# More combined images, some direct images normalised by VectorE, and weight steps in even portions, in a grouped convolution after a group norm

## The chip, the cores and the metric

The kernel runs on one core of a Trainium2 chip. A core has TensorE (matmuls into PSUM; PE in the profile, with PEld for its weight loads), VectorE (DVE), ScalarE (ACT), GpSimd (POOL) and SyncE (SP), which here issues most DMA transfers. Each engine works through its own queue in order; semaphores tie the queues together. The metric is the device time of one execution in microseconds (us). Durations of single instructions come from one profiled execution.

## What is computed

```python
# x: (160, 128, 32, 32) f32;  U: (5, 128*128*9) f32
s1 = (U.max() - U.min()) / 3;  v1 = s1 * floor(U / s1)
s2 = s1 / 5;                   v2 = s2 * floor((U - v1) / s2)
w  = (v1 + v2).reshape(128 * 5, 128, 3, 3)

def gn(v):                     # 32 groups of 4 channels over an image
    g = v.reshape(B, 32, 4, H, W)
    return (g - mean(g)) / sqrt(var(g) + 1e-5)

xb  = gn(x).reshape(32, 5 * 128, 32, 32)
act = conv(xb, w, 3x3, stride 1, padding 1, groups=5)
out = x + act.reshape(160, 128, 32, 32)
```

So there are five weight sets; each is applied to 32 of the 160 images. Every image is normalised, convolved 3x3 over 128 channels, and added to itself.

## The kernel before, in words

The 128 channels lie on the partitions. The kernel takes the images set by set (`place`), two images to a chunk of `xpool`. Matmuls are in f16, with the f32 data split into a high and a low part so that precision is kept. Per image there are these stages:

- **Load and statistics.** SyncE loads a chunk `LOAD_LEAD` = 20 images ahead. ScalarE measures an image 14 ahead with two passes (`image_sum`, L192; `image_square`, L199); eight early images are measured by VectorE (`BY_VECTOR`). GpSimd and two tiny matmuls turn eight images' sums into `rstd` and `shift`.
- **Direct images** (even ones from image 8 on). ScalarE writes z = x·rstd + shift (L510), then the f16 high part hi (L518). VectorE writes the low part lo = z - hi (L573) and combines its rows: differences two rows apart, sums and differences of row pairs (`combinations`, L587, L589, L590). TensorE convolves hi with the nine taps (L613, 18 matmuls over 512 columns, about) and the combined rows of lo with four combined weights per column of taps (L651, 6 of 512 and 12 of 256).
- **Combined images** (odd ones from `STEADY` = 7 on). The row combinations are formed on the raw x in f32: the outer rows on GpSimd (`outer_rows`, L538, L539), the rest on VectorE (`combine`, L549, L552, L555), 2048 values per partition in v. ScalarE scales v into vh (L560), VectorE into vl = v·rstd - vh (L566). TensorE needs no direct taps: 12 matmuls of 512 columns and 24 of 256 (L651).
- **The pair sums m.** For either kind `sums_of_pairs` lets TensorE first write the products of row sums and row differences to m, two PSUM banks. ScalarE copies the second bank to SBUF (`leave`, L709). VectorE writes their sum and difference into the rows of the output accumulator eo (`pairs`, L719, L721), and TensorE adds the remaining products on top (`rest_of_column`). `ps_m` has one buffer, `ps_eo` two.
- **Output.** ScalarE halves eo into `sum` (L735); GpSimd issues a DMA that adds it to the image in SBUF (L748); SyncE stores the chunk (L753).

The weights of the next set are quantised by VectorE meanwhile: `make_column` is a generator whose 14 steps for each of the three columns are taken one by one (`take(later, 1)`), 42 in all, from the third image of a set to its 29th (for the first set, from the fifth).

The order of every queue is written out by hand in `run`. In iteration i of the main loop the queues get:

- TensorE: m of i+1, then the rest of image i;
- ScalarE: the first pass over a new image, the output sum of i-1, the copy of m(i+1), z and hi or vh of i+3, the second pass;
- VectorE: the low part of i+2, L719 and L721 for i+1 (with a step or the last of three row combinations between them), the combine of i+4, and a step of the weights;
- GpSimd: the DMA issue for i-1, the outer rows of i+4, pieces of the statistics and weights;
- SyncE: the store of the chunk that ends in i-2, and loads.

Of the kernel before, what the change touches and what calls it, by code (L numbers as in the profile page):

```python
# [8 lines left out]
F32 = mybir.dt.float32  # L9
I32 = mybir.dt.int32  # L10
MM = mybir.dt.float16
ALU = mybir.AluOpType
# [297 lines left out]
class Main:  # L310
# [22 lines left out]


    STAT_LEAD = 14
    LOAD_LEAD = 20
    STEADY = 7
    BY_VECTOR = (8, 10, 11, 14, 19, 24, 29, 34)
    EARLY = 8
    FIRST = 3  # L340

# [4 lines left out]
    def __init__(self, tc, ctx, keep, x, u, out):  # L346
        nc = self.nc = tc.nc
        self.imgs, C, self.H, self.W = x.shape
        P = self.P = nc.NUM_PARTITIONS
        assert C == P and self.H * self.W == 1024  # L350
        self.per_set = self.imgs // N_SETS
        self.xv = x.rearrange("(b n) c h w -> n c b (h w)", n=N_SETS)
        self.ov = out.rearrange("(b n) c h w -> n c b (h w)", n=N_SETS)
        self.uv = u.rearrange("n (o i k) -> n o i k", o=C, k=TAPS)

        def pool(name, bufs, **kw):
            return ctx.enter_context(tc.tile_pool(name=name, bufs=bufs, **kw))

        self.const = pool("const", 1)
        self.qpool = pool("quant", 1)  # L360
        self.wpool = pool("weights", 2)
        self.upool = pool("u", 1)
        self.xpool = pool("x", 12)
        self.zpool = pool("z", 3)
        self.parts = pool("parts", 5)
        self.rows = pool("rows", 4)
        self.wide = pool("wide", 1)
        self.wide_parts = pool("wide_parts", 2)
        self.evac = pool("evac", 2)
        self.sums = pool("sums", 4)  # L370
        self.unread = pool("unread", 1)
        self.small = pool("small", 3)
        self.ps_eo = pool("ps_eo", 2, space=PSUM)
        self.ps_m = pool("ps_m", 1, space=PSUM)
        self.ps_stat = pool("ps_stat", 1, space=PSUM)
        self.ps_tr = pool("ps_tr", 1, space=PSUM)
        self.steps = Steps(nc, keep)
        self.chunks, self.z, self.hi, self.v, self.eo, self.m = {}, {}, {}, {}, {}, {}
        self.sum = {}
        self.wts = {}  # L380
        self.columns = []

        cuts = [0, 2, 4, 8, 12, 16, 20, *range(24, self.imgs + 1, 8)]
        self.groups = [range(a, b) for a, b in zip(cuts, cuts[1:])]
        self.group_of = {i: k for k, g in enumerate(self.groups) for i in g}
        self.stats = {}
# [118 lines left out]
    def normalise(self, i):  # L505
# [7 lines left out]
        )  # L513
        self.z[i] = z

    def high_part(self, i):
        hi = self.parts.tile([self.P, self.H, self.W], MM, tag="hi", name=f"hi{i}")
        self.nc.scalar.copy(hi.rearrange("p h w -> p (h w)"), self.z[i])  # L518
        self.hi[i] = hi

    def combined(self, i):

        return self.STEADY <= i < self.imgs and i % 2 == 1

    def column_of(self, i):

# [230 lines left out]
    def run(self):  # L757
# [39 lines left out]
        def take(steps, count):  # L797
            for _ in range(count):
                next(steps, None)

        def measure(stage, *images):
            for i in images:
                self.measure(i, (stage,))
# [68 lines left out]
        later, turned = iter(()), []  # L872
        for i in range(self.imgs):
            n, b = self.place(i)


            def on_the_way(col):
                if col == self.COLS[1]:
                    for st in ready:
                        st.means()  # L880
                    for *column, parts in self.columns:
                        turned.append((column, self.turn_column(*column, parts)))
                    self.columns.clear()
                if col == self.COLS[2]:
                    for st in middle:
                        st.variances()

            if i < self.FIRST:
                if i == self.FIRST - 1:
                    self.sums_of_pairs(self.FIRST)  # L890

                j = (i - 1) % self.FIRST
                self.direct_hi(j, self.COLS[2])
                self.direct_lo(j, self.COLS[2])
                if i == 0:
                    self.stats[2].variances()
                    self.stats[2].deviation()
                    self.stats[2].scales()
                for col in self.COLS:
                    on_the_way(col)  # L900
            else:
                j = i - 1
                self.conv(i, on_the_way)
            ahead = i + min(10 + i // 4, self.STAT_LEAD + 1)
            to_measure = range(measured, min(self.imgs, ahead))
            measured += len(to_measure)
            if n + 1 < N_SETS:
                if b == (2 if n == 0 else 0):
                    self.load_set(n + 1)
                if b == (4 if n == 0 else 2):  # L910
                    later = (s for col in self.COLS for s in self.make_column(n + 1, col))
            by_scalar = [k for k in to_measure if not self.by_vector(k)]
            by_vector = [k for k in to_measure if self.by_vector(k)]

            if i < self.FIRST:

                if i == 0:
                    measure(0, 8, 9, 10)
                    self.normalise(4)
                    self.high_part(4)  # L920
                if i == 2:
                    self.leave(3)
                    self.normalise(5)
                    measure(1, 9)
                    self.high_part(5)
                    self.pairs(3)
                    self.low_part(4)
                    run(self.combinations(4))
                self.residual(j)
                if i == 1:  # L930
                    measure(0, 11)
            else:

                rows = iter(())
                if self.combined(i + 2):
                    self.low_combined(i + 2)
                elif i + 2 < self.imgs:
                    self.low_part(i + 2)
                    take(later, 1)
                    rows = self.combinations(i + 2)  # L940
                    take(rows, 2)
                if i > self.FIRST and self.by_hand(j):
                    self.residual(j)
                for k in by_scalar:
                    self.measure(k, (0,))
                if i > self.FIRST and not self.by_hand(j):
                    self.residual(j)
                    self.accumulate(j)
                if self.combined(i + 4):
                    self.outer_rows(i + 4)  # L950


                part = i + 3 < self.imgs and not self.combined(i + 3)
                if i + 1 < self.imgs:
                    self.leave(i + 1)
                if part:
                    self.normalise(i + 3)
                    self.high_part(i + 3)
                if self.combined(i + 3):
                    self.high_combined(i + 3)  # L960
                for k in by_scalar:
                    self.measure(k, (1,))
            for st in middle:
                st.deviation()
                st.scales()
            for st in ready:
                st.deviations()
            for column, pt in turned:
                self.keep_column(*column, pt)
            turned = []  # L970

            if i >= self.FIRST:

                if i + 1 < self.imgs:
                    self.pairs(i + 1, lambda: take(rows if i % 2 == 0 else later, 1))
                run(rows)
                if self.combined(i + 4):
                    self.combine(i + 4)
                else:
                    take(later, 1)  # L980
                if b == self.per_set - 4:
                    run(later)

            middle, ready = ready, []
            if i >= self.FIRST:
                measure(0, *by_vector)
            for k in to_measure:
                group = self.group_of[k]
                if k + 1 == self.groups[group].stop:
                    ready.append(self.stats[group])  # L990
            self.store(i - 2)
            while loaded * NB < min(self.imgs, i + self.LOAD_LEAD):
                self.load(loaded)
                loaded += 1
# [49 lines left out]
```

## Time and profile before

| | |
|---|---|
| time, median of 3 runs | 1002.48 us (1001.89 to 1003.06) |
| span of the profiled execution | 1000.1 us, TensorE clock at 0.999 of full speed |
| images combined / not combined | 77 / 83 |
| DMA traffic | 254.42 MB, mean 254 GB/s |
| load of a chunk, issue to landing | median 9.0 us |
| added output, issue to landing | median 6.9 us, longest 11.8 |

The main loop runs from about 60 us to 990 us of the span: 157 images, 5.92 us each. Busy time of an engine is the union of its instructions; instructions of one engine overlap by some tens of ns, so that starts, not durations, are to be added up. In the slices of the page a digit is a tenth of a slice of 25 us. A wait is shown as "waiting instruction <- what ended the wait: total, times, longest". In a timeline the number in brackets is the idle time of that engine just ahead of the instruction.

### The profile page before, as it was taken

What the parts mean: (1) busy time and instruction counts of PE and PEld (TensorE: products, weight loads), DVE (VectorE), ACT (ScalarE), POOL (GpSimd) and SP (SyncE); (2) the same over time, 40 slices, a digit from 0 to 9 for tenths busy, and PEclk for the clock granted to TensorE, in tenths of its full rate; (3) what the DMA queues carried; (4) which work ended last, traced back from release to release, by engine and by line L of the source; (5) the groups of instructions that cost most, each with busy time, mean ns of one, the idle gap of its engine ahead of it and who ended that gap; (6) DMA issues with size and microseconds to landing.
All of it is one profiled execution on the core that took longest, in us unless ns stands there. A gap on an engine that the chain in (4) does not pass through costs nothing.

```text
span 1000.1 us, 15977 instructions
## 1 busy us (share of the span) xinstructions
PE 962.5 (96%) x5935; PEld 575.1 (58%) x5935; DVE 895.6 (90%) x1237; ACT 913.2 (91%) x1243; POOL 405.3 (41%) x575
## 2 busy tenths in 40 slices
PE   1999999999999999999999999999999999999997
PEld 0445555565655565666655566666565666666554
DVE  7999999998999999989999998999999988888884
ACT  4879999999999999999999999999999999998560
POOL 3435473553425262524364443426353523233310
PEclk9999999999999999999999999999999999999999
DMA  9628989999999999999989999999999999988773
GB/s 357 247 89 229 257 221 279 269 268 267 272 273 269 266 258 273 288 274 269 264 243 288 270 265 278 277 273 249 266 272 270 279 262 275 274 230 219 177 179 141
DMA packets 67287, 254.42 MB, mean 254 GB/s; under 512 B 5248, under 2 KB 5248, under 8 KB 67200
## 3 DMA queue, kind: packets, MB, share of 16 engines
q1 hardware_dynamic: 45168, 173.09, 50.2%
q0 software_dynamic: 22032, 80.23, 41.4%
q8 instruction: 48, 0.79, 0.3%
q14 instruction: 39, 0.32, 0.1%
HBM read 89.19 MB, written 83.89 MB: 173 GB/s over the span
## 4 chain that ended last, share of the span: by engine, by line
PE 73%; DVE 10%; ACT 10%; issue 3%; POOL 3%; DMA 1%; SPq 0%; DVEq 0%; POOLq 0%
PE eo L613 25%; PE m L651 25%; PE eo L651 22%; ACT junk L199 2%; ACT vh L560 2%; ACT sum L735 1%; ACT m L709 1%; DVE eo L719 1%; DVE eo L721 1%; ACT z L510 1%; ACT junk L192 1%; DVE lo L573 1%; DVE vl L566 1%; DMA range<-in_L_conv_U_dram 1%; DVE ext L421 1%
## 5 line engine op out<-in xcount | busy, mean ns | idle before, releaser
L651 PEld LDWEIGHTS <-wt 128*128 128x128 f16 x4212 | 409.0, 98 | 241.3 <-DVE eo L721 12.9
L613 PE MATMUL eo<-hi,wt 128*128 128x496 f16 (+1 forms) x1476 | 352.5, 375 | 1.1 <-ACT wt L475 0.6
L748 POOL DMA_DIRECT2D xt<-sum x153 | 136.5, 895 | 419.4 <-ACT sum L735 403.5
L613 PEld LDWEIGHTS <-wt 128*128 128x128 f16 x1548 | 151.3, 99 | 147.4 <-ACT wt L475 1.8
L566 DVE SCALAR_TENSOR_TENSOR vl<-v,rstd,vh 128x2048 f16<-128x2048 f32 x77 | 180.8, 2348 | 4.2 <-ACT vh L560 4.2
L651 PE MATMUL m<-vh,wt 128*128 128x496 f16 (+1 forms) x462 | 175.7, 380 | 5.2 <-DVE eo L721 4.6
L719 DVE TENSOR_TENSOR eo<-m,m 128x512 f32<-128x512 f32 x157 | 109.0, 695 | 77.8 <-ACT m L709 77.8
L651 PE MATMUL eo<-vl,wt 128*128 128x256 f16 (+1 forms) x924 | 177.1, 273 | 0.0
L651 PE MATMUL eo<-vh,wt 128*128 128x256 f16 (+1 forms) x924 | 177.1, 273 | 0.0
L651 PE MATMUL m<-vl,wt 128*128 128x496 f16 (+1 forms) x462 | 175.4, 380 | 0.0
L199 ACT ACTIVATE junk<-xt,mv 128x1024 f16<-128x1024 f32 x152 | 174.0, 1145 | 0.2
L192 ACT ACTIVATE junk<-xt 128x1024 f16<-128x1024 f32 x152 | 160.6, 1057 | 14.7 <-DMA xt<-in_x_dram 11.6
L735 ACT ACTIVATE sum<-eo 128x1024 f32<-128x1024 f32 x153 | 154.1, 1007 | 13.7 <-PE eo L651 13.7
L560 ACT ACTIVATE vh<-v,rstd 128x2048 f16<-128x2048 f32 x77 | 155.0, 2013 | 1.8 <-POOL v L539 1.8
L651 PE MATMUL eo<-rows,wt 128*128 128x248 f16 (+1 forms) x960 | 144.3, 273 | 0.0
L651 PE MATMUL m<-rows,wt 128*128 128x496 f16 (+1 forms) x480 | 116.9, 380 | 0.5 <-DVE eo L721 0.5
L709 ACT COPY m<-m 128x512 f32<-128x512 f32 x157 | 91.3, 582 | 27.4 <-PE m L651 23.9
L721 DVE TENSOR_TENSOR eo<-m,m 128x512 f32<-128x512 f32 x157 | 108.4, 691 | 1.0
L510 ACT ACTIVATE z<-xt,shift,rstd 128x1024 f32<-128x1024 f32 x83 | 103.2, 1243 | 3.5 <-POOL shift L242 3.5
L573 DVE TENSOR_TENSOR lo<-z,hi 128x1024 f16<-128x1024 f32 x83 | 101.5, 1223 | 0.0
L518 ACT CAST hi<-z 128x1024 f16<-128x1024 f32 x83 | 86.8, 1046 | 2.6
L549 DVE TENSOR_TENSOR v<-xt 128x960 f32<-128x960 f32 x77 | 88.4, 1149 | 0.0
(111 smaller groups left out, 863.3 us busy)
## 6 DMA issues: line engine op xcount, KB each, us to landing
xt<-in_x_dram SPq DMA_DIRECT2D x78, 1024.0 KB, 9.0
out_dram<-xt SPq DMA_DIRECT2D x78, 1024.0 KB, 5.2
xt<-sum POOLq DMA_DIRECT2D x153, 512.0 KB, 6.9
range<-in_L_conv_U_dram SPq DMA_DIRECT2D x4, 576.0 KB, 7.9
u<-in_L_conv_U_dram SPq DMA_DIRECT2D x4, 576.0 KB, 11.8
xt<-in_x_dram SPq DMA_DIRECT2D x4, 512.0 KB, 10.6
out_dram<-xt SPq DMA_DIRECT2D x3, 512.0 KB, 2.7
u<-in_L_conv_U_dram SPq DMA_DIRECT2D x2, 288.0 KB, 3.0
```

Of the source, the lines that this page charges most:

```text
L192: self.nc.scalar.activation(junk, image, ACTF.Copy, scale=-1.0 / image.shape[1], accum_out=self.mv[:, j, 0:1],)
L199: self.nc.scalar.activation(junk, image, ACTF.Square, bias=self.mv[:, j, 0:1], accum_out=self.mv[:, j, 1:2],)
L510: nc.scalar.activation(z, self.image(i), ACTF.Identity, bias=st.shift[:, j : j + 1], scale=st.rstd[:, j : j + 1],)
L560: self.nc.scalar.mul(vh, self.v[i], st.rstd[:, j])
L566: self.nc.vector.scalar_tensor_tensor(vl, self.v[i], st.rstd[:, j], self.hi[i], ALU.mult, ALU.subtract)
L573: self.nc.vector.tensor_sub(lo[:, 1 : self.H + 1, :].rearrange("p h w -> p (h w)"), self.z.pop(i), self.hi[i].rearrange("p h w -> p (h w)"),)
L613: nc.tensor.matmul(target[:, h, r0 - h0 : r1 - h0, c0:c1], self.wts[n, col][:, k, :], tile[:, s0 : s0 + r1 - r0, c0 + dw : c1 + dw], start ...
L651: self.nc.tensor.matmul(target[:, :, c0:c1], self.wts[n, col][:, kind, :], source[:, :, c0 + dw : c1 + dw], start=start, stop=stop, skip_g ...
L719: nc.vector.tensor_add(rows[:, :, 0], m[:, 0], m2)
L721: nc.vector.tensor_sub(rows[:, :, 1], m[:, 0], m2)
L735: nc.scalar.mul(self.sum[i], eo, 0.5)
L748: self.nc.gpsimd.dma_start(self.image(i), self.sum.pop(i), accum_op=ALU.add)
```

## The change

More of the images take the combined form: instead of every second one, four of each seven up to image 125 (positions 0, 2, 4, 6 of the seven, so that two follow each other where sevens meet), and two of each three from image 126 on. That is for TensorE, which has fewer columns to stream in a combined image. Of the direct images that are left, one in seven up to image 125 and all from 126 on have z written by VectorE instead of ScalarE (27 in all), for ScalarE's sake. Weight steps are taken in even portions: beside those at fixed places, a count due at the end of each iteration is made up. Two combined images in a row need two `wide` buffers and three `wide_parts`; to make room the x pool goes from 12 chunks to 11 with a lead of 18, and `sums` from 4 to 3.

```diff
-    LOAD_LEAD = 20
+    LOAD_LEAD = 18
+    THIRDS = 126
...
-        self.xpool = pool("x", 12)
+        self.xpool = pool("x", 11)
...
-        self.wide = pool("wide", 1)
-        self.wide_parts = pool("wide_parts", 2)
+        self.wide = pool("wide", 2)
+        self.wide_parts = pool("wide_parts", 3)
...
-        self.sums = pool("sums", 4)
+        self.sums = pool("sums", 3)
...
+    def normalise_by_vector(self, i):
+        st, j = self.column_of(i)
+        z = self.z[i] = self.zpool.tile([self.P, 1024], F32, tag="z", name=f"z{i}")
+        self.nc.vector.tensor_scalar(
+            z, self.image(i), st.rstd[:, j], st.shift[:, j], ALU.mult, ALU.add
+        )
+
+    def by_vector_too(self, i):
+        if i < self.STEADY + 4 or i >= self.imgs or self.combined(i):
+            return False
+        return i >= self.THIRDS or (i - self.STEADY) % 7 == 3
...
     def combined(self, i):
-        return self.STEADY <= i < self.imgs and i % 2 == 1
+        if i < self.STEADY or i >= self.imgs:
+            return False
+        return (i - self.STEADY) % 7 % 2 == 0 if i < self.THIRDS else i % 3 != 1
...
+        def steps_due(b, first):
+            last = self.per_set - 5
+            return 0 if b < first else 42 * (b - first + 1) // (last - first + 1)
...
                 if part:
-                    self.normalise(i + 3)
+                    if not self.by_vector_too(i + 3):
+                        self.normalise(i + 3)
                     self.high_part(i + 3)
...
-                    self.pairs(i + 1, lambda: take(rows if i % 2 == 0 else later, 1))
+                    self.pairs(i + 1, lambda: take(later if self.combined(i + 2) else rows, 1))
                 run(rows)
                 if self.combined(i + 4):
                     self.combine(i + 4)
-                else:
-                    take(later, 1)
+                elif self.by_vector_too(i + 4):
+                    self.normalise_by_vector(i + 4)
+
+                take(later, steps_due(b, 4 if n == 0 else 2) - self.step)
```

More of the change, by code (lines that the diff above doesn't have):

```diff
@@ L380, in __init__ @@
         self.wts = {}
+        self.step = 0
         self.columns = []
@@ L799, in take, with counted @@
                 next(steps, None)
+        def counted(steps):
+            self.step = 0
+            for step in steps:
+                self.step += 1
+                yield step
+        def steps_due(b, first):
+            last = self.per_set - 5
+            return 0 if b < first else 42 * (b - first + 1) // (last - first + 1)
         def measure(stage, *images):
@@ L910, in run @@
                 if b == (4 if n == 0 else 2):
-                    later = (s for col in self.COLS for s in self.make_column(n + 1, col))
+                    later = counted(
+                        s for col in self.COLS for s in self.make_column(n + 1, col)
+                    )
             by_scalar = [k for k in to_measure if not self.by_vector(k)]
```

## The prediction

> **What bounds the kernel now.** First the busy table and the slices of the page, for the balance of the engines:
>
> ```profile
> PE 962.5 (96%) x5935; PEld 575.1 (58%) x5935; DVE 895.6 (90%) x1237; ACT 913.2 (91%) x1243; POOL 405.3 (41%) x575
> ...
> PE   1999999999999999999999999999999999999997
> ...
> DVE  7999999998999999989999998999999988888884
> ACT  4879999999999999999999999999999999998560
> ```
>
> TensorE, VectorE and ScalarE are all nearly full; VectorE has room only in the last slices, where no weights are made. Then the waits, to see who is late:
>
> ```profile
> DVE eo L719 <- ACT m L709: 77.8, 77, 2.0
> ...
> PEld L651 <- DVE eo L721: 12.9, 31, 1.5
> PE m L651 <- DVE eo L721: 5.0, 10, 1.2
> ```
>
> They form a ring. TensorE writes m(i+1); ScalarE copies half of it (L709); VectorE adds and subtracts (L719, L721); only then may TensorE write m(i+2), because `ps_m` has one buffer. So what counts is the rhythm from image to image. The timeline of one pair of images shows it (start, duration, engine, line, idle before):
>
> ```profile
> 511.06 0.39 PE L651 MATMUL m<-vh,wt 128*128 128x512 f16 x1 [0.17 <-DVE eo L721]
> ...
> 514.50 0.58 ACT L709 COPY m<-m 128x512 f32<-128x512 f32 x1
> ...
> 516.74 0.68 DVE L721 TENSOR_TENSOR eo<-m,m 128x512 f32<-128x512 f32 x1
> ...
> 518.79 1.46 PE L651 MATMUL m<-rows,wt 128*128 128x512 f16 x6
> ...
> 520.29 0.59 ACT L709 COPY m<-m 128x512 f32<-128x512 f32 x1
> ...
> 520.91 0.70 DVE L719 TENSOR_TENSOR eo<-m,m 128x512 f32<-128x512 f32 x1 [0.97 <-ACT m L709]
> ...
> 522.18 0.69 DVE L721 TENSOR_TENSOR eo<-m,m 128x512 f32<-128x512 f32 x1
> ```
>
> The next m starts at 522.92, 0.05 after VectorE's end: the pair takes 11.86 us, of which TensorE was held 0.17. Near 890 us, where no weights are made, a pair takes 11.64 (m starts at 889.15 and 900.79) with no stall.
>
> [...] 12 matmuls of m take 2.61 (511.06 to 513.67), 0.217 each, and L721 has a mean of 691. [...]
>
> **The change, part by part.** C is a combined image, D a direct one.
>
> TensorE. C needs 12 matmuls for m and 24 half-size ones: 2.60 + 2.66 = 5.26. D takes 1.30 for m and 5.12 for the rest (513.67 to 518.79): 6.42. There were 77 C, now 68 + 23 = 91: 14 x 1.16 = **16.2 us less TensorE work**.
>
> VectorE, start to start in the trace: combine (L549, L552, L555) 2.34; vl 2.28; lo and its three rows 1.13+0.60+0.33+0.33 = 2.39; the two ops on m 1.21; a weights' step 0.48 on average (14 rows of 0.34 to 0.75, less overlap). C costs 2.34+2.28-2.39 = 2.23 more than D: 14 x 2.23 = **31 us more**. The new z is an fp32 `tensor_scalar` from SBUF, 1024 wide, 27 times; no row shows it. [...] I take 0.65: 18 us more.
>
> ScalarE: 27 z at 1.24 go, 34 us; C costs 1.9 against 2.23 for z and hi. From one copy of m to the next it needs, start to start, copy 0.47, vh 1.90 (or z 1.28 + hi 0.95), square 1.27, sum 1.06, output sum (L735) 0.93: **5.68 for C, 6.0 for D**, 4.73 for D with z on VectorE.
>
> So per seven images: TensorE 4 x 5.26 + 3 x 6.42 = 40.3, VectorE 4 x 4.62 + 3 x 2.39 + 7 x 1.21 + 0.65 = 34.8, with 11 steps x 0.48 = 40.1, ScalarE 39.5. No total exceeds TensorE's, but VectorE has nothing left for waiting, and the order inside the seven matters.
>
> The ring, image by image. M = start of m(i+1) on TensorE, A = end of its copy, D = end of L721:
> - next M = later of M + P and D + 0.05. P is what TensorE has in iteration i, m(i+1) and then the rest of image i: 1.30 + 2.66 = 3.96 for C before D, 2.60 + 5.12 = 7.72 for D before C, 2.60 + 2.66 = 5.26 for C before C.
> - A = later of previous A + V (ScalarE's work between two copies, set by the kind of image i+2) and M + 2.1 where image i+1 is D (518.79 to 520.88), M + 3.4 where it is C (1.3 more matmuls).
> - D = later of previous D + W (VectorE's queue) and A + 1.33 + what stands between L719 and L721: a step 0.48 or rows 0.33.
>
> W holds, in the queue's order, combine(i+3) or z(i+3), the low part of i+2 (vl or lo with rows), the two ops on m, and 0.78 of steps (42 over 26 images, at 0.48). So combine+lo+ops is 5.94, vl+ops 3.49, combine+vl+ops 5.83, each plus 0.78. The sequence is C D C D C D C and again C, r = (i-7) mod 7. I start from M = 0 with the last A at -1.80 and the last D at -0.05, about where the table ends:
>
> | r | P | V | W | M | A | D |
> |---|---|---|---|---|---|---|
> | 0 | 3.96 | 5.68 | z+vl 4.92 | 0 | 3.88 | 5.69 |
> | 1 | 7.72 | 4.73 | 6.72 | 5.74 | 9.14 | 12.41 |
> | 2 | 3.96 | 5.68 | 4.27 | 13.46 | 15.55 | 17.36 |
> | 3 | 7.72 | 6.00 | 6.72 | 17.42 | 21.55 | 24.08 |
> | 4 | 3.96 | 5.68 | combine+vl 6.61 | 25.14 | 27.23 | 30.69 |
> | 5 | 7.72 | 5.68 | 4.27 | 30.74 | 34.14 | 35.95 |
> | 6 | 5.26 | 6.00 | 6.72 | 38.46 | 41.86 | 43.52 |
>
> The next M is 43.72. TensorE is held 1.78 after r0, since two copies after adjacent C come 3.96 apart and ScalarE needs 5.68, and 1.64 after r4, since VectorE has combine and vl in one short image. Before, 3.5 pairs took 41.5: **+2.2 per seven**. The same rules give 11.7 for the old pair (measured 11.86), so they do not exaggerate. Without steps they give 41.6 against 3.5 x 11.64 = 40.7: +0.9. With two of three combined the crossing comes every three images, with W = 2.34+2.28+1.21 = 5.83 where TensorE has 3.96: in the C before C iteration D is M + 3.4 + 1.33 + 0.33 = M + 5.06; the next D is 5.83 later, so the M after that cannot come before M + 10.94, where TensorE alone needs 5.26 + 3.96 = 9.22. The three take 16.94 + 1.72 = 18.66 against 1.5 x 11.64 = 17.46: **+1.2**.
>
> Sum: steps run during 99 of images 7 to 125, 14.1 sevens x 2.2 = +31; the other 20, 2.9 x 0.9 = +2.6; the end, some 10 threes x 1.2 = +12. Together +46: **1048**. The z estimate hardly enters[...].
>
> Costs put at nothing: the second `wide` and third `wide_parts` buffer serve adjacent C. `sums` 4 to 3: reuse comes three images later, 17 us; the transfer lands in 6.9 us, at most 11.8. `xpool` 11 and lead 18: issue to first use falls from five images to three, about 18 less 5 us of SP's lateness = 13; loads between 300 and 800 us land in 7.2 to 11.8. Hidden, narrowly. Even portions replace a burst of few steps: already in W.
>
> **The rivals.**
> 1. *TensorE stays the bound.* For it: the totals fit, and ScalarE is relieved. Then 16.2 go, and with them some 3 of the 17.9 us of waits shown above: 983. Against it: one m buffer cannot carry slack from long images into short ones. 12%.
> 2. *Half of the stalls.* If VectorE's steps happen to fall into the long images, the hold after r4 goes: 43.72-1.64 = 42.1, +0.6 x 14.1 = +8; with the other two terms 1025. 14%.
> 3. *Late loads as well.* If a third of 70 chunks hold ScalarE 0.7 us, +16: 1064. It would be slower than the main case: 5%.
>
> Main case 67%, no change 2% (between 1 and 2). Range 1018 to 1064: it leaves out case 1, no change, and the edges. Faster 0.12, same 0.03, slower 0.85.
>
> **What would show it.** Right: m waiting for L721 much longer than 17.9 us in all, in gaps of 1.5 us or so, twice in seven images and once in three at the end; L719 waiting for L709 after adjacent C; TensorE below 93% busy, though with 91 C. ScalarE under 88%. Wrong: m's starts 40 us apart per seven, or ScalarE waiting for loads.

## The result and the profile after

| | before | changed |
|---|---|---|
| time, median | 1002.18 us (1001.58 to 1003.06, 4 runs) | 1054.99 us (1054.01 to 1056.44, 4 runs) |
| ratio | 1 | 1.0527, 95% interval 1.0509 to 1.0546 |
| span of the profiled execution | 1000.1 us | 1053.8 us |

The change makes the kernel 53 us slower; 1048 was forecast. In the changed file the lines have moved: L709 is L727 (ScalarE's copy of m), L719 and L721 are L737 and L739 (VectorE's add and subtract), L651 is L669 (products), L566 is L584 (vl), L735 is L753 (output sum). The busy table and the slices of the changed kernel's page:

```profile
PE 955.8 (91%) x5935; PEld 574.3 (54%) x5935; DVE 943.6 (90%) x1264; ACT 883.2 (84%) x1202; POOL 439.8 (42%) x603
...
PE   1989998799999899999999999999999999898996
...
DVE  7999997998899999889999998899999988889885
ACT  4879897789889998998998989988999888877451
```

No engine is full any more: TensorE has less work than before and is busy for 91%, VectorE 48 us more than before and still 90%, ScalarE 30 us less. Eights appear in rows that were nines. The waits (waiting line, what ended the wait: us in all, times, longest) say what the engines do instead:

```profile
ACT m L727 <- PE m L669: 95.2, 84, 7.1
DVE eo L737 <- ACT m L727: 82.0, 83, 2.4
PEld L669 <- DVE eo L739: 74.9, 51, 6.3
PE m L669 <- DVE eo L739: 61.0, 41, 6.0
```

TensorE's wait for VectorE before m rose from 5.0 to 61.0 us. In the row of its weight loads it rose from 12.9 to 74.9; these are the same gaps, measured from the end of the last weight load, and must not be added to the others. ScalarE's wait for m rose from 23.9 to 95.2; in the kernel before its row is

```profile
ACT m L709 <- PE m L651: 23.9, 28, 4.7
```

All four waits are one ring: TensorE m, ScalarE copy, VectorE add and subtract, TensorE m. On TensorE this nearly adds up to the loss: 56.0 us more of waits before m and 6.7 us less of busy time are 49 of the 53 us. The start times of the subtract of an image give the loss by stage:

| images | before, us | changed, us | difference | forecast |
|---|---|---|---|---|
| to 7 | 86.8 | 87.3 | +0.5 | 0 |
| 7 to 28 | 127.3 | 142.2 | +14.9 | +6.6 (3 sevens with steps) |
| 28 to 126 | 580.1 | 606.8 | +26.7 | +27.0 (11.1 sevens with steps, 2.9 without) |
| 126 to 156 | 175.6 | 188.0 | +12.4 | +12 (10 threes) |

One seven of the changed kernel (images 56 to 63), as the chain of waits walks it, in order of time (start, us, what); the chain goes back from the last instruction and changes engine wherever another released it:

```profile
402.32 2.00 ACT vh L578
...
406.64 0.91 ACT sum L753
407.55 0.48 ACT m L727
...
408.06 0.70 DVE eo L737
...
409.74 2.77 PE m L669 x12
...
417.63 1.31 PE m L669 x6
418.96 0.59 ACT m L727
...
421.41 1.06 DVE v L567
...
424.20 1.13 DVE lo L591
...
428.13 1.06 DVE v L567
...
430.92 2.26 DVE vl L584
433.18 0.62 DVE eo L737
433.82 0.71 DVE eo L739
...
434.58 2.77 PE m L669 x12
```

Before, the chain from 511 to 540 us is all PE but for the issue. Here it leaves TensorE twice. From 402 to 408 it is ScalarE, which has to do vh, a second and a first pass and the output sum before the copy of the next m, as two combined images have just met. From 419 to 434.5 it is VectorE's queue without a gap: combine, lo, the two ops, combine again and vl. Two timeline lines show what TensorE pays (in brackets its idle time):

```profile
409.74 0.39 PE L669 MATMUL m<-vh,wt 128*128 128x512 f16 x1 [1.39 <-DVE eo L739]
434.58 0.39 PE L669 MATMUL m<-vh,wt 128*128 128x512 f16 x1 [0.94 <-DVE eo L739]
```

These are the two places in seven that the table of the prediction has (r0 and r4).

### The profile page after: what moved, and what is told of

It is laid out like the page before. It is cut to its first block, busy times and chain, and to the rows that moved or that the text cites. A ratio compares the mean times of both kernels' runs of the same rounds, so it can differ in the third digit from the quotient of the medians.

```text
span 1053.8 us, 16029 instructions
## 1 busy us (share of the span) xinstructions
PE 955.8 (91%) x5935; PEld 574.3 (54%) x5935; DVE 943.6 (90%) x1264; ACT 883.2 (84%) x1202; POOL 439.8 (42%) x603
## 3 DMA queue, kind: packets, MB, share of 16 engines
q0 software_dynamic: 22032, 80.23, 39.4%
## 4 chain that ended last, share of the span: by engine, by line
PE 45%; DVE 33%; ACT 11%; issue 4%; POOL 4%; DMA 2%; SPq 0%; POOLq 0%; ACTq 0%; DVEq 0%
PE m L669 20%; PE eo L631 16%; PE eo L669 6%; DVE vl L584 6%; DVE eo L737 5%; DVE eo L739 5%; DVE v L567 4%; ACT vh L578 3%; ACT junk L199 3%; DVE v L570 3%; DVE v L573 2%; ACT m L727 2%; DVE lo L591 2%; DMA xt<-sum 1%; ACT sum L753 1%
## 5 line engine op out<-in xcount | busy, mean ns | idle before, releaser
L669 PEld LDWEIGHTS <-wt 128*128 128x128 f16 x4464 | 432.8, 98 | 311.8 <-DVE eo L739 74.9
L631 PE MATMUL eo<-hi,wt 128*128 128x496 f16 (+3 forms) x1224 | 292.4, 376 | 1.1 <-ACT wt L477 0.6
L669 PE MATMUL m<-vh,wt 128*128 128x512 f16 x546 | 209.9, 384 | 60.3 <-DVE eo L739 60.2
L584 DVE SCALAR_TENSOR_TENSOR vl<-v,rstd,vh 128x2048 f16<-128x2048 f32 x91 | 213.6, 2347 | 0.4 <-ACT vh L578 0.3
L669 PE MATMUL eo<-vh,wt 128*128 128x256 f16 (+1 forms) x1092 | 209.3, 273 | 0.0
L669 PE MATMUL eo<-vl,wt 128*128 128x256 f16 (+1 forms) x1092 | 209.3, 273 | 0.0
L669 PE MATMUL m<-vl,wt 128*128 128x512 f16 x546 | 209.3, 383 | 0.0
L578 ACT ACTIVATE vh<-v,rstd 128x2048 f16<-128x2048 f32 x91 | 182.7, 2007 | 4.9 <-POOL v L557 4.0
L737 DVE TENSOR_TENSOR eo<-m,m 128x512 f32<-128x512 f32 x157 | 109.2, 696 | 82.3 <-ACT m L727 82.0
L753 ACT ACTIVATE sum<-eo 128x1024 f32<-128x1024 f32 x153 | 154.6, 1011 | 26.4 <-PE eo L669 25.6
L192 ACT ACTIVATE junk<-xt 128x1024 f16<-128x1024 f32 x152 | 160.7, 1057 | 17.3 <-DMA xt<-in_x_dram 14.3
L727 ACT COPY m<-m 128x512 f32<-128x512 f32 x157 | 91.4, 582 | 96.0 <-PE m L669 95.2
L669 PE MATMUL eo<-rows,wt 128*128 128x248 f16 (+1 forms) x792 | 119.1, 273 | 0.0
L739 DVE TENSOR_TENSOR eo<-m,m 128x512 f32<-128x512 f32 x157 | 108.8, 693 | 1.2
L669 PE MATMUL m<-rows,wt 128*128 128x496 f16 (+1 forms) x396 | 96.5, 380 | 0.8 <-DVE eo L739 0.8
L557 POOL TENSOR_SCALAR v<-xt,ngm 128x32 f32<-128x32 f32 x91 | 82.5, 907 | 0.0
L556 POOL TENSOR_SCALAR v<-xt,ngm 128x32 f32<-128x32 f32 x91 | 80.3, 883 | 0.0
```

What stands on the lines that cost most here:

```text
L192: self.nc.scalar.activation(junk, image, ACTF.Copy, scale=-1.0 / image.shape[1], accum_out=self.mv[:, j, 0:1],)
L578: self.nc.scalar.mul(vh, self.v[i], st.rstd[:, j])
L584: self.nc.vector.scalar_tensor_tensor(vl, self.v[i], st.rstd[:, j], self.hi[i], ALU.mult, ALU.subtract)
L631: nc.tensor.matmul(target[:, h, r0 - h0 : r1 - h0, c0:c1], self.wts[n, col][:, k, :], tile[:, s0 : s0 + r1 - r0, c0 + dw : c1 + dw], start ...
L669: self.nc.tensor.matmul(target[:, :, c0:c1], self.wts[n, col][:, kind, :], source[:, :, c0 + dw : c1 + dw], start=start, stop=stop, skip_g ...
L727: self.nc.scalar.copy(m2, self.m[i][:, 1])
```

## The experiments

**Five sizes alone.** Are the smaller pools the cause?

```diff
-    LOAD_LEAD = 20
+    LOAD_LEAD = 18
-        self.xpool = pool("x", 12)
+        self.xpool = pool("x", 11)
...
+        self.wide = pool("wide", 2)
+        self.wide_parts = pool("wide_parts", 3)
+        self.sums = pool("sums", 3)
```

> The kernel before with only the five sizes of the change: x pool 11 chunks, lead 18, sums 3, wide 2, wide_parts 3; same images combined as before. Theory A (the rhythm of the ring through the one m buffer makes the loss): none of these is on the ring, so 1002 us, within 3. Theory B (the shorter lead and the smaller pools make loads and buffers late): a good part of the 53 us, 1015 to 1055, with ScalarE waiting for xt from DMA.

Measured: 1005.02 us beside 1002.07, ratio 1.0029 (1.0019 to 1.0039). ScalarE's wait for loads went from 11.6 us in 2 times to 18.0 in 8. So the sizes that the prediction put at nothing cost 3 us in the old rhythm, with the waits for loads as the likely way; they are not the 53.

**z back on ScalarE.** Is it VectorE's new work?

```diff
     def by_vector_too(self, i):
...
-        return i >= self.THIRDS or (i - self.STEADY) % 7 == 3
+        return False
```

> The changed kernel with z of every direct image written by ScalarE, as before (the 27 VectorE ones of 0.81 us, 22 us in sum, go; ScalarE gets 27 x 1.28 = 34 us more). Theory A: after the adjacent combined images the add waits for ScalarE's copy whether z is there or not, and the next images have slack on ScalarE, so 1055 us, within 5. Theory C (VectorE simply has too much work, whatever the order): its load falls by 2%, so 1033 to 1040.

Measured: 1050.96 us, ratio 1.0494 (1.0477 to 1.0512). Within theory A's bound, and 4 us better. By stage the gain lies before image 28 (135.3 us instead of 142.2); from 28 to 126 it is 2 us slower (609.1), from 126 to 156 equal (187.8). VectorE is busy for 18 us less and ScalarE for 28.5 us more; in the steady sevens this exchange buys nothing.

**The order alone.** As many combined images as before, but C C D D.

```diff
-        return (i - self.STEADY) % 7 % 2 == 0 if i < self.THIRDS else i % 3 != 1
+        return (i - self.STEADY) % 4 < 2
...
-        return i >= self.THIRDS or (i - self.STEADY) % 7 == 3
+        return False
```

> The changed code with as many combined images as before (77), but in the order C C D D instead of C D C D, z on ScalarE. Totals of work on each engine are those of before. Theory A: the same table gives 26.2 us for four images with steps (23.7 before) and 25.2 without (23.3): 24.8 x 2.4 + 13.5 x 1.9 = +86, so 1088 us, 1075 to 1095. Theory C (sums of work decide): 1002 to 1006.

Measured: 1123.72 us, ratio 1.1218 (1.1195 to 1.1242). VectorE and ScalarE have the work that they had before (897.5 and 920.5 us busy, within 1%), and the time rises by 121 us. The five sizes and the even portions of steps are still those of the change; but from image 126 on there are no steps, and there the stage takes 190.5 us instead of 175.6, four images 25.4 us where the table gives 25.2. So the order by itself makes a loss, more than the whole change does. With steps four images take 27.3 us where the table gives 26.2, and that is most of the 36 us by which the forecast fell short. Half pace, which the table leaves out, may be a large part of that (last section).

**Three banks for m, first try (e4_three_banks).** To take the ring away, m was given three banks in one tile, statistics and weight transposes sharing a bank.

```diff
+        self.m3 = self.ps_m.tile([P, 3, self.H // 2, self.W], F32, tag="m3", name="m3")
...
-        m = self.m[i] = self.banks(self.ps_m, "m", i)
+        m = self.m[i] = self.m3[:, i % 2], self.m3[:, 2]
```

> The changed kernel with m in three PSUM banks: the half that VectorE reads alternates between two banks, the half that ScalarE copies keeps one; statistics and weight transposes share one bank to make room. TensorE no longer waits for VectorE before the next m. Theory A: the holds after r0 and r4 and those at the crossings of the threes go; some 41 us per seven and 17.1 per three, so 990 to 1005 us. Theories B and C: the waits only move to the accumulator, 1045 to 1055.

Measured: 1063.62 us, ratio 1.0616 (1.0598 to 1.0634), a miss for theory A's number, and not a test of it: the wait was still there. The waits of this kernel (its own line numbers, L675 and L745 for the products and the subtract):

```profile
PE m L675 <- DVE eo L745: 61.3, 43, 6.0
...
PE few L213 <- DVE big L81: 6.9, 1, 6.9
```

61.3 us as against 61.0: here the instructions on the one tile still waited for each other, whatever bank they touched. The second line, a statistic that waits at the start behind the shared bank, accounts for most of the 8 us more: up to image 7 this kernel takes 93.4 us instead of 87.3.

**Tiles of their own (e8_own_tiles).** So the two halves of m became separate tiles; only the half that VectorE reads has two buffers. Statistics and weight transposes share one bank, as in the last try.

```diff
-        self.ps_m = pool("ps_m", 1, space=PSUM)
+        self.ps_ma = pool("ps_ma", 2, space=PSUM)
+        self.ps_mb = pool("ps_mb", 1, space=PSUM)
...
+    def two(self, i):
+        return self.bank(self.ps_ma, "ma", i), self.bank(self.ps_mb, "mb", i)
...
-        m = self.m[i] = self.banks(self.ps_m, "m", i)
+        m = self.m[i] = self.two(i)
```

> The changed kernel with the two halves of m as tiles of their own: the half that VectorE reads has two buffers, the half that only ScalarE copies has one; statistics and weight transposes share one bank. In e4_three_banks the three banks were one tile, and TensorE's wait for VectorE before m stayed as it was (61 us); here m waits for ScalarE's copy, and VectorE's result is needed one m later (1.3 to 2.6 us of slack). Theory A: the table with that slack gives 40.4 to 41 us per seven images and 16.9 per three: 985 to 1000 us. Theory C (VectorE has too much work in whatever order): 1040 to 1055.

Measured: 1025.01 us, ratio 1.0223 (1.0188 to 1.0259). 30 of the 53 us come back, so the ring is the larger part; the time is still 25 to 40 us over the forecast. The wait of m for the subtract is gone, and others are in its place:

```profile
ACT junk L192 <- DMA xt<-in_x_dram: 33.3, 14, 11.4
...
PE ma L683 <- DVE vl L590: 16.9, 21, 4.0
...
PEld few L230 <- POOL dv L227: 16.2, 12, 3.7
```

ScalarE waits for loads, TensorE for vl and for the statistics on GpSimd. By stage, images 126 to 156, where the loads end and no weights are made, take 173.6 us, less than before the change (175.6): there the ring was everything. Between images 28 and 126 the sevens are uneven: the best take 40.5 to 41.5 us, the worst 45 to 46, where those of the changed kernel take 41.9 to 44.3. In all that stage takes 599.9, against 606.8.

**The same tiles in the kernel before.**

> The kernel before with the same tiles for m as e8_own_tiles. Theory A: its holds were small (17.9 us of waits), and ScalarE is 98% full: 992 to 1001 us, a small gain.

Measured: 996.38 us, ratio 0.9947 (0.9931 to 0.9964): the old rhythm with a free ring is the best kernel of the study, faster than both.

**Sevens to the end.**

```diff
-    THIRDS = 126
+    THIRDS = 160
```

> The changed kernel with four of seven combined to the end (no two of three). Theory A: the crossing of adjacent combined images then comes 5 times after image 126 instead of 11 times: from the trace +12.4 us there, which becomes about +4: 1045 to 1049 us. Theory C: VectorE's and TensorE's totals change by under 1% at the end, so 1053 to 1057.

Measured: 1045.83 us, ratio 1.0448 (1.0428 to 1.0469), as theory A has it. Images 126 to 156 take 176.4 us instead of 188.0. Six fewer meetings of combined images give 11.6 us back there, although fewer images are combined.

**Statistics off VectorE at the start.**

```diff
-    BY_VECTOR = (8, 10, 11, 14, 19, 24, 29, 34)
+    BY_VECTOR = (8, 10, 11)
```

> The changed kernel in which only images 8, 10 and 11 are measured by VectorE; 14, 19, 24, 29 and 34 go to ScalarE. In the trace images 7 to 28 lost 15 us where the table gives 7. Theory A, VectorE's statistics (about 1.75 us an image) stand in the full VectorE queue there: 1046 to 1051 us. Rival: ScalarE (2.33 us an image) is what is late there: 1057 to 1065.

Measured: 1056.91 us, ratio 1.0556 (1.0537 to 1.0574). Both expectations missed the point: 7 to 28 take 140.8 us instead of 142.2. Neither engine's statistics explain the slow start.

**No weights' steps (e10_no_steps).** This kernel leaves out the quantising of the other four sets; the first set's weights serve all.

```diff
-                    later = counted(
-                        s for col in self.COLS for s in self.make_column(n + 1, col)
-                    )
+                    for col in self.COLS:
+                        self.wts[n + 1, col] = self.wts[0, col]
```

> The changed kernel without the weights' steps of sets 1 to 4: the first set's weights are used for all (left out: the quantising of the other four sets, 80 us of VectorE). m still has one buffer. Theory A (order and ring): the table without steps gives 41.6 per seven images where 43.35 was measured, so 24 us less between images 28 and 126 and some 5 before: 1025 us, 1018 to 1030. Theory C (VectorE was simply full, and now is not): the sevens reach TensorE's 40.3: 1000 to 1008.

Measured: 1025.44 us, ratio 1.0233 (1.0216 to 1.0251), at the table's value. VectorE's busy time is 70.5 us less than in the changed kernel (ScalarE's 10, GpSimd's 68). The sevens from 28 to 126 take 41.8 us (41.6 by the table), not TensorE's 40.3. Even with VectorE at 85% the ring holds TensorE: its waits for the subtract before m are still 39.4 us. This parts the loss of the sevens: some 1.5 of 3 us over TensorE's sum belong to the steps, above all in VectorE's full queue, the rest to the order.

**No steps and tiles of their own.**

> e8_own_tiles without the weights' steps of sets 1 to 4 (the same part left out as in e10_no_steps). Neither the ring nor a full VectorE is left, so if these two are all that holds TensorE, it runs at 40.3 to 40.7 per seven and 17 per three: 980 to 990 us. If late loads and late statistics are what held e8_own_tiles at 1025, they hold this one as well: 1000 or more.

Measured: 998.31 us, ratio 0.9964 (0.9952 to 0.9976). Above the 980 to 990 that the two causes alone would leave: 28 to 126 take 578.5 us (41.3 per seven, 40.3 was expected). Its profile still has ScalarE waiting 30.5 us for loads, and TensorE 9.5 for the statistics. These are the candidates for the rest.

**Room for the loads.** The x pool back at 12 with lead 20, in the kernel with tiles of their own.

```diff
-    LOAD_LEAD = 18
+    LOAD_LEAD = 20
-        self.xpool = pool("x", 11)
-        self.zpool = pool("z", 3)
-        self.parts = pool("parts", 5)
+        self.xpool = pool("x", 12)
+        self.zpool = pool("z", 2)
+        self.parts = pool("parts", 4)
...
-        ident = self.const.tile([P, P], F32, tag="ident", name="ident")
+        ident = self.space("ident")[:, 0, :P]
```

> e8_own_tiles with the x pool back at 12 chunks and a lead of 20; room comes from z (3 to 2 buffers), the direct high parts (5 to 4) and the identity matrix. In e8_own_tiles ScalarE waited 33 us for loads, where 14 did in the changed kernel. If those waits are on the path: 1006 to 1015 us. If VectorE and the statistics hold it: 1021 to 1028.

Measured: 1018.16 us, ratio 1.0166 (1.0149 to 1.0183), between the two expectations. ScalarE's wait for loads fell by 22 us, from 33.3 to 11.3, all but a trace of it at the start; 7 us of this were gained in time, net of what the smaller pools for z and the high parts may cost.

**One image's z.** z of image 24 alone returns to ScalarE.

```diff
-        return i >= self.THIRDS or (i - self.STEADY) % 7 == 3
+        return i != 24 and (i >= self.THIRDS or (i - self.STEADY) % 7 == 3)
```

> The changed kernel in which z of image 24 alone goes back to ScalarE. In the trace VectorE's z of image 24 waited 3.9 us for its group's shift, TensorE was then idle for 6.0 us and ran the next m at half pace. If that one wait is what images 7 to 28 lost beyond the table (15.4 against about 7, most of it after image 21): 1047 to 1050 us. If not: 1055.

Measured: 1049.78 us, ratio 1.0470 (1.0453 to 1.0488), 5 us under the changed kernel. The step from image 21 to image 22 falls from 10.5 to 6.7 us, and in the two profiles no other step up to image 35 differs by more than 0.3. What that wait looked like in the changed kernel's timeline:

```profile
184.60 0.81 DVE L521 TENSOR_SCALAR z<-xt,rstd,shift 128x1024 f32<-128x1024 f32 x1 [3.94 <-POOL shift L242]
...
191.25 0.61 PE L669 MATMUL m<-vh,wt 128*128 128x512 f16 x1 [6.02 <-DVE eo L739]
```

VectorE writes z one image earlier than ScalarE did. Image 24 is the first of its group, and that group's shift was only just coming from GpSimd; behind z stood a statistic, vl and the two ops on m, and behind these TensorE.

## Why the prediction was right, and where it was off

**The rhythm.** The table held image by image. Time from one subtract to the next, for the seven from 403.40 to 446.66 us:

| r | 0 | 1 | 2 | 3 | 4 | 5 | 6 | sum |
|---|---|---|---|---|---|---|---|---|
| table (differences of D) | 5.89 | 6.72 | 4.95 | 6.72 | 6.61 | 5.26 | 7.57 | 43.72 |
| trace | 5.60 | 6.99 | 4.73 | 6.72 | 6.38 | 4.92 | 7.92 | 43.26 |

TensorE was held 1.39 us after r0 (1.78 forecast) and 0.94 after r4 (1.64). The mean seven between 28 and 126 took 43.35, and a three 18.80 (18.66 forecast). The experiments show the mechanism and not only its size: the order alone makes the loss (C C D D), fewer meetings make it smaller (sevens to the end), and giving TensorE a buffer's slack returns 30 us.

**The work.** VectorE's busy time rose by 48.0 us, 49 was summed. z came out at 812 ns on average (0.73 start to start), above the 0.65 taken, which was the author's estimate and stood in no trace. All but two of the 27 took 0.80 to 0.82 us and the longest 0.89. ScalarE's busy time fell by 30, less than the 39 of the sums. TensorE's fell by 6.7, not 16.2: half pace (last section) puts back 3 us, and 31 more waits by estimate some 5, since the last matmul before a wait shows its whole 0.38 us where in a run the next starts after 0.217.

**The steps that were off.**
- *"The z estimate hardly enters."* In the steady rhythm that holds: at r0 in the table VectorE's queue is 0.82 us short of setting D, so that z would have to take more than 1.47. But a queue instruction is not only its length: the new z also waits, and the prediction named no wait of it. Images 7 to 28 lost 14.9 us, not 6.6. z of image 24 is 4 us of that in the trace, 5 in the time; without any VectorE z the stage is at +8.0. The 3 us between these two profiles lie in the steps to images 20 and 24 (6.5 and 6.1 us with z of image 24 alone back on ScalarE, 5.0 and 4.5 with every z there). Both kernels have TensorE held there for the same 2.75 and 2.14 us; in the one it ran its next matmuls at half pace, in the other it did not (last section). So that part is the pace's and not z's own work, and 1.4 us stay unexplained.
- *"Hidden, narrowly"* for the loads: 3 us in the kernel before with the five sizes, about 7 us in the one with a free ring. In the changed kernel itself the waits for loads are 14.3 us, 11.3 of them one wait at the start, so there it held.
- *Rivals.* "Half of the stalls" put the whole weight on where the steps fall; without any steps the time is 1025, so nearly half of the loss comes from the order itself; that the rival's number was 1025 too is chance. "TensorE stays the bound" (983) did not come about even with free tiles and no steps (998).
- *Sums.* The 17.9 us of waits before count the same gaps twice; TensorE was held for 12.9. ScalarE's pieces for C add up to 5.63 and not 5.68, which moves the hold after r0 by 0.05. Of the signs, L719 waiting for L709 says little: its total rose only from 77.8 to 82.0 us.

**Open.** How the last 14 us of the kernel with free tiles and no steps (578.5 against 14 x 40.3 = 564 between images 28 and 126) divide between loads, statistics and copies was not taken apart; half pace may have a share too, since the mean granted clock of that profile is 0.993 (last section). That the loads are part of it is shown only for the kernel with steps. The even portions of steps were not run by themselves, so what they add in the sevens with steps is not known; where there are no steps, the order makes its loss without them.

## What to carry to other kernels

Where one buffer is handed round three engines, add up each engine's queue per step of the ring, not per kernel: 16 us of matmuls were saved here, every engine's total still fitted, and 53 us were lost, since long and short images no longer alternated and VectorE's queue had no slack left to make up for it. Before putting more work into such a ring, free it: two tiles in place of one gave 0.5% to the old kernel at once. An instruction that is moved to an earlier place in another queue brings its waits along; ask what it reads and when that is ready for the first item of a batch.

## What the runs showed of the hardware

After some long holds TensorE's next matmuls started 0.43 us apart instead of 0.217, at half pace. In the changed kernel this follows the hold of 6.02 us:

```profile
191.65 0.15 PEld L669 LDWEIGHTS <-wt 128*128 128x128 f16 x1 [0.28 <-issue]
192.08 0.15 PEld L669 LDWEIGHTS <-wt 128*128 128x128 f16 x1 [0.28 <-issue]
192.51 0.15 PEld L669 LDWEIGHTS <-wt 128*128 128x128 f16 x1 [0.28 <-issue]
```

It came after a hold of 2.75 us as well (at 166.07, from the fifth matmul on), and not after holds of 1.39 and 0.94. The granted clock that this trace records is 0.50 from 166.74 to 170.15 us and from 187.22, 2.0 us into the hold of 6.02, to 194.05; from 31 to 1050 us it is 1.00 everywhere else. The hold's length alone does not decide: the kernel with z of image 24 on ScalarE and the one with every z there both have holds of 2.75 and 2.14 us near 166 and 186 us. After them the twelve matmuls of m took 3.99 and 4.28 us in the first and 2.60 and 2.61 in the second. What decides was not shown.

In the changed kernel TensorE worked for 3.41 and 2.80 us of the two stretches at 0.50. Half of that, 3.1 us, is by estimate what half pace cost it, all of it between images 7 and 28. In C C D D six matmuls of m took 2.53 us after a hold of 2.72 (at 436.07) and 1.31 after one of 2.48 (at 409.38). The mean granted clock is 0.976 over the whole of C C D D, 0.991 in the kernel with tiles of its own, 0.994 in the changed kernel, 0.999 before. From these numbers an upper estimate for C C D D is 0.023 of 1120.8 us, 26 us more than before; it counts the time in which TensorE was held as if it had worked. How it divides by stage, and how much of the 36 us by which the forecast fell short it is, was not shown. So a hold can cost more than its length, in the pair above 1.4 and 1.7 us of m, and the table did not have that. This may be part of why runs of one kernel differ: the four with z of image 24 on ScalarE took from 1046.99 us, at a mean granted clock of 0.999, to 1051.55, at 0.996.
